# Ends of an attention on VectorE, two blocks of the next projection at a time, and a batch norm's variance summed beside the attention

## The chip, the cores and the metric

The kernel runs on one core of a Trainium2 chip. The metric is the device time of one launch in microseconds. The time before is the median of three runs. All stages below run one after the other on the same core; its engines are TensorE (PE in the profile, with its weight loads PEld), VectorE (DVE), ScalarE (ACT), GpSimd (POOL) and SyncE (SP), which issues most of the plain transfers.

## The reference

A graph of N = 3327 nodes has 512 features a node (x) and a sparse 0/1 adjacency matrix (adj). Four layers follow, each as `x = x + layer(relu(layernorm(x)))`:

```
layer 0   attention (8 heads of 64), then batch norm over the nodes (mean, var), scale, shift, relu
layer 1   mean over neighbours (mask @ h / degree), two linear maps, concatenated, a third, relu
layer 2   attention (8 heads of 64), elu
layer 3   attention (8 heads of 64), elu

attention: Wh = h W;  e[i,j] = leaky_relu(s[i] + d[j]) where adj[i,j], else minus infinity
           out[i] = softmax_j(e[i,:]) @ Wh, head by head
batch norm: mean and var of the attention's output over all nodes, a value for each of 512 columns
```

## The kernel before

The nodes are padded to 3328 and held as 26 blocks of 128 rows (NB = 26). Since the adjacency is sparse, each group of 64 destination nodes (52 groups, two to a block) keeps a list of the source nodes that it needs, rounded up to chunks of 128. The table CAPS has the number of chunks of each group, 22 for the first down to 4 for the last; 359 chunks in all. Every stage that reads neighbours gathers the 359 chunks by an indirect DMA that GpSimd issues (`gather`, L1165), one chunk at a time, into tiles named rows (attentions) or z_rows (layer 1).

**Attention** (`attend`, L1170). The groups are cut into 135 units of two or three chunks. For a unit VectorE makes mx (L1266: the larger of two factors of the exponential, one from PSUM and one from the gathered rows) and wgt (L1273: mx times the 0/1 mask), and TensorE multiplies wgt with the gathered rows into facc (L1287). In the first attention VectorE also unpacks the mask's bits ("on", L1252) and ScalarE turns them into the mask (L1258). The gathered rows have six buffers, and the gathers of a unit are issued one unit ahead in the program; GpSimd may run further ahead, up to what the buffers allow.

When a group's last unit has gone through, its end is worked off in steps, one step for each following unit (`ending`, L1201): ScalarE copies facc to sums (L1215), VectorE takes the reciprocal of the row sums (rd, L1219), ScalarE scales eight pieces of 64 columns into the block's output (L1225, named bn_y in layer 0 and fhp later). After a block's second group come the steps of `finish`: for layers 2 and 3 the elu (fin_e, fin_x, L1314 to L1320).

At each unit `later()` moves every pending end on by one step and then calls `tick()`, the work beside the attention. PE, VectorE and ScalarE run in the order in which the program calls them (`manual_schedule`); GpSimd's and SP's order is made by the framework's scheduler.

**Beside the first attention** (`beside`, L1339). Each tick does a small piece: first two products of layer 1's weights, then the sum of the attention's output over the nodes, a block at a time, as a matmul with ones (bmean_ps, L1374). After the attention the mean is taken (L1376). The variance follows in a stage of its own (L1398 to L1407): for two blocks at a time VectorE subtracts the mean (bn_d), ScalarE squares, TensorE sums into var_ps; bn_var is the result. Then come the batch norm's scale and shift, the layer norm of layer 1 and one of its linear maps.

**Layer 1** gathers the 359 chunks again (z_rows), sums them on TensorE (sage_acc, L1522) and finishes a block in `ending` (L1459).

**Beside layers 1 and 2** the projection of the following attention is made, a block at a time, by the class `Following` (L740): `norm` (layer norm, ScalarE sums, squares and scales; the result is ln_h), then `rest_by_rows` (used beside layer 1, where the vectors `ab` are given) or `rest` (beside layer 2): transposes (p_ps), relu to hT, the product with the score weights (p_sd), the product with the weights (p_wh, L866), eight ScalarE scalings into v_row (L870), which goes to the table in memory, and the transposed scores (p_tr to r_row), which go to r_dram. `tick` advances the block in front by two steps when two are waiting, else by one:

```
for _ in range(min(2, len(self.ready))):
    while self.ready and next(self.ready[0]) is None:
        self.ready.pop(0)
```

All PSUM tiles of `rest` share one tag of two buffers. When the units of the attention are through, `while ends: later()` works off the last ends, and `proj.drain()` (L1534) the last blocks of the projection. The next attention's first gather needs the whole table.

Of the kernel before, what the change touches and what calls it, by code (L numbers as in the profile page):

```python
# [23 lines left out]
F32 = mybir.dt.float32  # L24
# [7 lines left out]
AF = mybir.ActivationFunctionType  # L32
# [6 lines left out]
P = 128  # L39
# [13 lines left out]
HALF = 64  # L53
BATCH = 4
WB = 16
LNB = 5
ROW = H * (F + 1) + H
UNIT = 3
# [681 lines left out]
class Following:  # L740
# [3 lines left out]
    def __init__(self, tc, cs, N, wl, W, WA, table, r_dram, pool, psum, pb=1, ab=None):  # L744

        self.__dict__.update(locals())
        nc = tc.nc
        if ab is not None:
            self.ab = pool.tile([P, 2, D], F32, name=f"ab{wl}")
            for k, a in enumerate(ab):  # L750
                nc.sync.dma_start(self.ab[:, k, :], a.partition_broadcast(P))
        self.NB = table.shape[0] // P
        self.Wt = pool.tile([P, KC, D], F32, name=f"fWt{wl}")
        nc.sync.dma_start(self.Wt, W.rearrange("(kc p) o -> p kc o", p=P))
        self.hs = pool.tile([P, self.NB, KC], F32, name=f"hs{wl}")
        self.early, self.ready = [], []

    def begin(self, c, xt):
        self.early.append(self.norm(c, xt))

    def tick(self):
        for _ in range(min(2, len(self.ready))):
            while self.ready and next(self.ready[0]) is None:
                self.ready.pop(0)
        for g in list(self.early):
            hx = next(g)
            if hx is not None:
                self.early.remove(g)
                self.ready.append((self.rest if self.ab is None else self.rest_by_rows)(*hx))
# [3 lines left out]
            self.tick()  # L773

    mean = Projection.mean

    def norm(self, c, xt):
        nc, pp, cs = self.tc.nc, self.pool, self.cs
# [62 lines left out]
    def rest(self, c, hx):  # L841
        nc, pp, WA, wl = self.tc.nc, self.pool, self.WA, self.wl
        tp = self.psum.tile([P, KC, P], F32, name="p_ps", tag="p_ps", bufs=self.pb)
        for kc in range(KC):
            nc.tensor.transpose(tp[:, kc, :], hx[:, kc * P : (kc + 1) * P], self.cs["ident"])
        hT = pp.tile([P, KC, P], F32, name="hT", tag="hT", bufs=2)
        for kc in range(KC):
            nc.scalar.activation(hT[:, kc, :], tp[:, kc, :], AF.Relu, accum_out=self.hs[:, c, kc : kc + 1])
        yield True
        self.mean(c, hT)  # L850
        sd = self.psum.tile([P, BANK], F32, name="p_sd", tag="p_ps", bufs=self.pb)
        for kc in range(KC):
            nc.tensor.matmul(sd[:, : 2 * H], hT[:, kc, :], WA[wl][:, kc, :], start=(kc == 0), stop=(kc == KC - 1))
        row = pp.tile([P, ROW], F32, name="v_row", tag="v_row", bufs=2)
        V = row[:, : H * (F + 1)].rearrange("p (h f) -> p h f", f=F + 1)
        d = sd[:, H : 2 * H]
        nc.scalar.activation(V[:, :, F : F + 1], d.rearrange("p (h o) -> p h o", o=1), AF.Exp)
        nc.scalar.activation(row[:, H * (F + 1) :], d, AF.Exp, scale=-0.8, bias=self.cs["down"])
        sf = pp.tile([P, H], F32, name="s_col", tag="s_col", bufs=2)
        nc.scalar.copy(sf, sd[:, :H])  # L860
        yield True

        nc.vector.tensor_scalar(sf, sf, -SMALL, SMALL, ALU.max, ALU.min)
        wh = self.psum.tile([P, D], F32, name="p_wh", tag="p_ps", bufs=self.pb)
        for kc in range(KC):
            nc.tensor.matmul(wh, hT[:, kc, :], self.Wt[:, kc, :], start=(kc == 0), stop=(kc == KC - 1))  # L866
        yield True
        rs = halves(nc, pp, self.cs, sf)
        for h in range(H):
            nc.scalar.mul(V[:, h, 0:F], wh[:, h * F : (h + 1) * F], V[:, h, F : F + 1])  # L870
        nc.sync.dma_start(self.table[c * P : (c + 1) * P, :ROW], row.bitcast(I32))
        yield True
        tr = self.psum.tile([2 * H, P], F32, name="p_tr", tag="p_ps", bufs=self.pb)
        nc.tensor.transpose(tr, rs(), self.cs["ident"])
        yield True
        rr = pp.tile([2 * H, P], F32, name="r_row", tag="r_row", bufs=2)
        nc.scalar.copy(rr, tr)
        n = P // GB
        nc.sync.dma_start(
            self.r_dram[c * n : (c + 1) * n, :, :, :].rearrange("g t h i -> (t h) g i"),  # L880
            rr.rearrange("h (g i) -> h g i", i=GB),
        )
        yield None
# [253 lines left out]
def sparse(ctx: ExitStack, tc: tile.TileContext, t: dict, out: bass.AP, WA, ls, cs, idx, rdeg, first):  # L1137
# [12 lines left out]
    def used(c):  # L1150
        return min(P, N - c * P)
# [15 lines left out]
        )  # L1167


    def attend(layer, table, r_dram, finish, tick=lambda: None, home=None):  # L1170

# [8 lines left out]
        with tc.tile_pool(name=f"fatt{layer}", bufs=2) as ap, tc.tile_pool(  # L1182
            name=f"facc_ps{layer}", bufs=2, space=PSUM
        ) as aps, tc.manual_schedule(engines={ET.PE, ET.DVE, ET.Activation}):
            rows, rrs, rbs, accs, ends = {}, {}, {}, {}, []

            def fetch(g):
                if g < ls.G:
# [12 lines left out]
            def ending(g, hps={}):  # L1201

                b, u = divmod(g, PG)
                if u == 0:
                    hps[b] = home[:, b, :] if home is not None else None
                    if home is None:
                        hp_ = ap.tile([P, D], F32, name="fhp", tag="hp", bufs=3)
                        hps[b] = hp_
                hp, o0 = hps[b], u * GB
                fin = finish(b, hp, ap)  # L1210
                if u == PG - 1:
                    next(fin)
                yield
                sm = ap.tile([P, sw], F32, name="sums", tag="sums", bufs=4)
                nc.scalar.copy(sm, accs.pop(g)[:, :sw])  # L1215
                sm = sm.rearrange("p (q x) -> p q x", x=F + 1)
                yield
                rd = ap.tile([P, hq, 1], F32, name="rd", tag="rd", bufs=4)
                nc.vector.reciprocal(rd, sm[:, :, F : F + 1])  # L1219
                yield  # L1220
                for v in range(PG):
                    mine = slice(v * GB, (v + 1) * GB)
                    for q in range(hq):
                        h = q * PG + v
                        nc.scalar.mul(hp[o0 : o0 + GB, h * F : (h + 1) * F], sm[mine, q, 0:F], rd[mine, q, :])  # L1225
                yield
                if u == PG - 1:
                    del hps[b]
                    yield from fin
# [31 lines left out]
            for i, (g, k0, n, begins, stops) in enumerate(units):  # L1261
# [31 lines left out]
                            )  # L1293
                if stops:
                    ends.append(ending(g))
            while ends:
                later()

    def following(lx, layer, wl, W, pb=1, ab=None):
# [30 lines left out]
    with ExitStack() as mx:  # L1330
# [8 lines left out]
        def beside(wp, wps):  # L1339
# [4 lines left out]
            for k, (wn, bn) in enumerate((("L1_WsT", "L1_gnn_b_self"), ("L1_WnT", "L1_gnn_b_nb"))):  # L1344
# [13 lines left out]
                for fc in range(KC):  # L1358
# [7 lines left out]
                    w = wp.tile([P, D], F32, name="fwx", tag="fwx", bufs=1)  # L1366
                    nc.scalar.copy(w, ps)
                    nc.sync.dma_start(wx_dram[k, fc, :, :], w)
            mean_ps = wps.tile([P, D], F32, name="bmean_ps", tag="beside", bufs=1)
            for c in range(NB):  # L1370
                while len(whole) <= c:
                    yield
                k = used(c)
                nc.tensor.matmul(mean_ps, ones[:k, :], y[:k, c, :], start=(c == 0), stop=(c == NB - 1))  # L1374
                yield
            nc.vector.tensor_scalar_mul(mean, mean_ps, 1.0 / N)  # L1376

        mean = mid.tile([P, D], F32, name="bn_mean")
        with tc.tile_pool(name="beside", bufs=1) as wp, tc.tile_pool(name="beside_ps", bufs=1, space=PSUM) as wps:
            bg = beside(wp, wps)  # L1380
# [14 lines left out]
        gps = mx.enter_context(tc.tile_pool(name="fsage_ps", bufs=2, space=PSUM))  # L1395
        two = [P, 2, D]
        with tc.tile_pool(name="fbn", bufs=1) as bp:
            var_ps = gps.tile([P, D], F32, name="var_ps", tag="n_ps")  # L1398
            for c in range(0, NB, 2):
                d = bp.tile(two, F32, name="bn_d", tag="bn_d", bufs=2)  # L1400
                nc.vector.tensor_tensor(d, y[:, c : c + 2, :], mean.unsqueeze(1).to_broadcast(two), ALU.subtract)
                nc.scalar.activation(d, d, AF.Square)
                for i in range(2):
                    k = used(c + i)
                    nc.tensor.matmul(var_ps, ones[:k, :], d[:k, i, :], start=(c + i == 0), stop=(c + i == NB - 1))
            var = bp.tile([P, D], F32, name="bn_var")
            nc.scalar.mul(var, var_ps, 1.0 / N)  # L1407
            nc.vector.tensor_tensor(gam, gam, rsqrt(nc, bp, cs, var, bufs=1)(), ALU.mult)
            nc.vector.tensor_tensor(mean, mean, gam, ALU.mult)
            nc.vector.tensor_tensor(bet, bet, mean, ALU.subtract)  # L1410
# [119 lines left out]
    with ExitStack() as l3:  # L1530
        at2 = proj
        proj = following(l3, 3, 2, t["L3_gnn_W"])
        attend(2, at2.table, at2.r_dram, elu_into(x2, x3, proj.begin), proj.tick)
        proj.drain()  # L1534
    attend(3, proj.table, proj.r_dram, elu_into(x3, out))


# [85 lines left out]
```

## Time and profile before

| what | us |
|---|---|
| median of three runs | 2559.43 (2559.01 to 2560.68) |
| the profiled execution: its own time | 2553.76 |
| its span | 2551.8 |
| lists and first projection | 0 to 319 |
| first attention | 319 to 806 |
| variance | 808 to 842 |
| batch norm, layer norm, first map of layer 1 | 842 to 930 |
| layer 1 | 930 to 1447 |
| second attention, with the last blocks of the next projection | 1447 to 2046 |
| third attention | 2046 to 2538 |

Busy time over the whole span: PE 1825.0 us (72%), VectorE 1852.3 (73%), ScalarE 1068.3 (42%), GpSimd 1387.4 (54%). These shares are means over stages that have different limits. What a part of the change is worth is read from the stage it lies in: which engine is full there, and which wait ends last. The profile counts a gather as busy for 0.95 us; what lies between two gathers shows as idle time before the second one, with the name of what ended it. "issue" there is time in which the engine waited for nothing that the profile shows.

### The profile page before, as it was taken

The numbers are of one execution on the slowest core, as the hardware profiler recorded it, in microseconds if no ns is written. First come the engines' busy times: TensorE is split into PE (matmuls) and PEld (weight loads), VectorE is DVE, ScalarE is ACT, GpSimd is POOL, SyncE is SP. The second block draws the span as 40 slices with busy tenths as digits, with TensorE's granted clock in tenths as the row PEclk, the third lists the DMA queues.
The fourth block names the chain that finished last, engine by engine and source line by source line (L and its number), as shares of the span: only waits on it lengthen the run. The fifth ranks groups of instructions, "written<-read, shape, count | busy, mean of one in ns | idle before, by whom it ended". The sixth has DMA issues, their size and how long they took to land.

```text
span 2551.8 us, 53690 instructions
## 1 busy us (share of the span) xinstructions
PE 1825.0 (72%) x21112; PEld 1161.8 (46%) x21112; DVE 1852.3 (73%) x2272; ACT 1068.3 (42%) x3810; POOL 1387.4 (54%) x1482
## 2 busy tenths in 40 slices
PE   3667756776677698889999657778878646566653
PEld 2444444454454342223333356656555435555543
DVE  7667579999997850222333499999877279999996
ACT  4553212333445332334455214667766601233444
POOL 1000176777772026777777277776554067777672
PEclk9767889988888899999999778897877787777787
DMA  8773198888783566788888478887665178888784
GB/s 326 288 263 123 43 296 276 280 281 260 241 253 95 191 217 198 234 247 260 254 267 255 125 223 242 235 240 232 199 200 177 39 215 232 236 238 243 232 238 123
DMA packets 189057, 562.57 MB, mean 220 GB/s; under 512 B 37764, under 2 KB 42304, under 8 KB 185470
## 3 DMA queue, kind: packets, MB, share of 16 engines
q0 software_dynamic: 115456, 404.86, 53.3%
q1 hardware_dynamic: 73342, 154.20, 17.0%
q8 instruction: 169, 2.77, 0.4%
q14 instruction: 90, 0.74, 0.1%
HBM read 499.26 MB, written 59.68 MB: 219 GB/s over the span
## 4 chain that ended last, share of the span: by engine, by line
PE 30%; DVE 24%; issue 13%; ACT 9%; DMA 8%; POOL 3%; DVEq 0%; SPq 0%; POOLq 0%; ACTq 0%
DVE mx L1266 12%; PE facc L1287 8%; DVE wgt L1273 8%; PE sage_acc L1522 4%; DMA z_rows<-h_dram,idx 4%; PE p_wh L866 4%; DMA rows<-table,idx 3%; PE n_ps L1471 3%; PE p_wh L808 3%; ACT fhp L1225 2%; POOL z_rows L1165 2%; PE s_ps L1445 2%; POOL rows L1165 1%; ACT bn_y L1225 1%; ACT v_row L870 1%
## 5 line engine op out<-in xcount | busy, mean ns | idle before, releaser
L1165 POOL DMA_INDIRECT rows<-table,idx x1077 | 1027.7, 954 | 580.0 <-issue 224.5
L1287 PE MATMUL facc<-rows,wgt 128*64 128x65 f32 x17232 | 722.5, 253 | 393.7 <-DVE wgt L1273 259.7
L1287 PEld LDWEIGHTS facc<-rows,wgt 128*64 128x64 f32 x17232 | 667.1, 165 | 518.2 <-DVE wgt L1273 310.5
L1266 DVE TENSOR_TENSOR mx<-r_bc,rows 128x1536 f32<-128x1536 f32 (+1 forms) x405 | 639.4, 1579 | 48.4 <-DMA fin_x<-fx 17.7
L1273 DVE TENSOR_TENSOR wgt<-mx,mask 128x1536 f32<-128x1536 f32 (+1 forms) x405 | 638.4, 1576 | 42.3 <-DVE mx L1266 1.0
L1165 POOL DMA_INDIRECT z_rows<-h_dram,idx x359 | 340.7, 949 | 273.7 <-ACT hT L1442 141.0
L1225 ACT ACTIVATE fhp<-sums,rd 64x64 f32<-64x64 f32 x832 | 219.9, 334 | 305.4 <-DVE rd L1219 302.0
L1522 PE MATMUL sage_acc<-z_rows,z_mask 128*64 128x512 f32 x718 | 209.8, 618 | 33.0 <-DMA z_rows<-h_dram,idx 32.6
L1258 ACT ACTIVATE mask<-on 128x192 uint8<-128x192 uint16 (+1 forms) x135 | 46.5, 345 | 325.3 <-DVE on L1252 321.8
L1086 POOL DMA_DIRECT2D list_b<-shift x12 | 6.0, 503 | 271.7 <-DVE shift L1040 271.5
L811 DVE TENSOR_TENSOR sd_pr<-p_wh,ab 128x1024 f32<-128x1024 f32 x26 | 31.8, 1225 | 141.4 <-PE p_wh L808 141.4
L1522 PEld LDWEIGHTS sage_acc<-z_rows,z_mask 128*64 128x64 f32 x718 | 52.2, 137 | 156.2 <-issue 77.6
L680 PE MATMUL wh_ps<-fWt,hT 128*128 128x512 f32 x208 | 123.3, 748 | 0.0
L866 PE MATMUL p_wh<-fWt,hT 128*128 128x512 f32 x208 | 117.2, 714 | 1.4 <-ACT s_col L860 1.4
L1225 ACT ACTIVATE bn_y<-sums,rd 64x64 f32<-64x64 f32 x416 | 109.5, 333 | 2.4 <-DVE rd L1219 0.5
L1503 ACT CAST z_mask<-mask 128x128 f32<-128x128 uint8 (+1 forms) x196 | 52.7, 284 | 118.7 <-PE sage_acc L1522 117.5
L1476 DVE TENSOR_TENSOR s_o<-n_ps,bn_y 128x512 f32<-128x512 f32 x26 | 17.9, 690 | 116.2 <-PE n_ps L1471 116.2
L1215 ACT COPY sums<-facc 128x260 f32<-128x260 f32 x156 | 56.6, 363 | 104.7 <-DMA rows<-table,idx 77.7
L1471 PE MATMUL n_ps<-fWx,aT 128*128 128x512 f32 x208 | 98.7, 608 | 0.0
L808 PE MATMUL p_wh<-fWt,hT 128*128 128x512 f32 x208 | 96.9, 610 | 2.0 <-DVE hT L699 1.9
L1445 PE MATMUL s_ps<-fWx,hT 128*128 128x512 f32 x208 | 93.5, 603 | 3.4 <-ACT hT L1442 3.4
L1198 PE MATMUL r_bc<-r_two,fones 2*128 2x512 f32 x156 | 89.1, 575 | 6.6 <-DMA r_two<-r_dram 3.6
(213 smaller groups left out, 2146.3 us busy)
## 6 DMA issues: line engine op xcount, KB each, us to landing
adj_i<-in_adj SPq DMA_DIRECT2D x26, 1664.0 KB
table<-v_row SPq DMA_DIRECT2D x78, 264.0 KB
rows<-table,idx POOLq DMA_INDIRECT x1077
fin_x<-fx SPq DMA_DIRECT2D x52, 256.0 KB
ln_x<-in_x SPq DMA_DIRECT2D x26, 256.0 KB
bn_x<-in_x SPq DMA_DIRECT2D x13, 512.0 KB
fx<-bn_x SPq DMA_DIRECT2D x13, 512.0 KB
fsage_x<-fx SPq DMA_DIRECT2D x26, 256.0 KB
```

The costliest lines, as they stand in the source:

```text
L680: nc.tensor.matmul(wh, hT[:, kc, :], self.Wt[:, kc, :], start=(kc == 0), stop=(kc == KC - 1))
L808: nc.tensor.matmul(wh, hT[:, kc, :], self.Wt[:, kc, :], start=(kc == 0), stop=(kc == KC - 1))
L866: nc.tensor.matmul(wh, hT[:, kc, :], self.Wt[:, kc, :], start=(kc == 0), stop=(kc == KC - 1))
L1165: nc.gpsimd.indirect_dma_start(out=dst, out_offset=None, in_=src[:, :], in_offset=bass.IndirectOffsetOnAxis(ap=idx[:, k : k + 1], axis=0))
L1198: nc.tensor.matmul(rb, ones[0:2, :].bitcast(F32R), rrs.pop(g).bitcast(F32R), start=True, stop=True)
L1225: nc.scalar.mul(hp[o0 : o0 + GB, h * F : (h + 1) * F], sm[mine, q, 0:F], rd[mine, q, :])
L1266: nc.vector.tensor_tensor(mx[:, :n], rbs[g].unsqueeze(1).to_broadcast(full), gt[:, :n, H * (F + 1) : ROW].unsqueeze(3).to_broadcast(full), ...
L1273: nc.vector.tensor_tensor(wt[:, :n], mx[:, :n], mk.unsqueeze(2).to_broadcast(full), ALU.mult)
L1287: nc.tensor.matmul(accs[g][v * GB : (v + 1) * GB, q * (F + 1) : (q + 1) * (F + 1)], wt[:, k, h, :], gt[:, k, h * (F + 1) : (h + 1) * (F + 1)],
L1445: nc.tensor.matmul(ps, hT[:, kc, :], Wx[:, 0, kc, :], start=(kc == 0), stop=(kc == KC - 1))
L1471: nc.tensor.matmul(ps, aT[:, kc, :], Wx[:, 1, kc, :], start=(kc == 0), stop=(kc == KC - 1))
L1522: nc.tensor.matmul(acc[u * GB : (u + 1) * GB, :], m, z, start=f, stop=l)
```

## The change

There are four parts.

1. **Ends after the last unit.** Once all units of an attention are through (`over`), an end that has not begun yet is done by VectorE alone: the reciprocal straight from facc in PSUM, and two products of 64 rows by 256 columns into the output, in place of ScalarE's copy and eight scalings. Ends that are already under way go on as before. This holds for all three attentions.
2. **Two blocks at a time.** After the last unit of the second attention the projection of the third is told to `hurry`: the three PSUM banks of mx become its banks (one each for p_sd, p_wh and p_tr), a tick moves two blocks by one step each, VectorE makes v_row in one instruction instead of ScalarE in eight, and the remaining norms use `norm_by_columns`. The drain is now part of the attention's loop, and so in the program's order.
3. **Norm by columns.** `norm_by_columns` does the layer norm on VectorE with bn_stats, bn_aggr and one tensor_scalar; it takes one step less than `norm`. All 26 blocks beside layer 1 use it.
4. **Variance beside the first attention.** `beside` sums, in one PSUM tile, the output (lower 64 rows) and the squares of its distance from a shift (upper 64 rows). The shift is the mean of the first eight blocks (NSHIFT); GpSimd subtracts it, ScalarE squares, TensorE sums, one step of each in a tick. Up to four blocks are under way. At the end the mean and the variance are put together from the two sums. The variance stage is gone.

```
@@ class Following @@
     def begin(self, c, xt):
-        self.early.append(self.norm(c, xt))
+        self.early.append((self.norm_by_columns if self.spare is not None or self.ab is not None else self.norm)(c, xt))
+    def bank(self, shape, name, k):
+        if self.spare is not None:
+            return self.spare[: shape[0], k, : shape[1]]
+        return self.psum.tile(shape, F32, name=name, tag="p_ps", bufs=self.pb)
     def tick(self):
+        if self.spare is not None:
+            for g in self.ready[:2]:
+                if next(g) is None:
+                    self.ready.remove(g)
+            self.step()
+            return
...
+    def norm_by_columns(self, c, xt):
+        nc.vector.bn_stats(st, xt)
+        nc.vector.bn_aggr(mv, st)
+        step = rsqrt(nc, pp, cs, mv[:, 1:2])
+        yield
+        y = step()
+        hx = pp.tile([P, D], F32, name="ln_h", tag="ln_h", bufs=3)
+        nc.vector.tensor_scalar(hx, xt, mv[:, 0:1], y, ALU.subtract, ALU.mult)
+        yield c, hx
...
@@ rest @@
-        for h in range(H):
-            nc.scalar.mul(V[:, h, 0:F], wh[:, h * F : (h + 1) * F], V[:, h, F : F + 1])
+        if self.spare is not None:
+            nc.vector.tensor_tensor(
+                V[:, :, 0:F], wh.rearrange("p (h f) -> p h f", f=F), V[:, :, F : F + 1].to_broadcast([P, H, F]), ALU.mult
+            )
+        else:
+            for h in range(H):
+                nc.scalar.mul(V[:, h, 0:F], wh[:, h * F : (h + 1) * F], V[:, h, F : F + 1])
...
@@ attend: ending @@
+                if over:
+                    sm = accs.pop(g)[:, :sw].rearrange("p (q x) -> p q x", x=F + 1)
+                    rd = ap.tile([P, hq, 1], F32, name="rd", tag="rd", bufs=4)
+                    nc.vector.reciprocal(rd, sm[:, :, F : F + 1])
+                    for v in range(PG):
+                        mine = slice(v * GB, (v + 1) * GB)
+                        nc.vector.tensor_tensor(
+                            hp[o0 : o0 + GB, :].rearrange("p (q v f) -> p q v f", v=PG, f=F)[:, :, v, :],
+                            sm[mine, :, 0:F], rd[mine].to_broadcast([GB, hq, F]), ALU.mult,
+                        )
...
@@ attend: after the units @@
-            while ends:
+            over.append(True)
+            if beside is not None:
+                mx = aps.tile([P, UNIT, H, GB], F32, name="mx", tag="mx", bufs=1)
+                beside.hurry(mx.rearrange("p k h i -> p k (h i)"))
+            while ends or (beside is not None and beside.busy()):
                 later()
@@ beside @@
-            for c in range(NB):
-                while len(whole) <= c:
-                    yield
-                nc.tensor.matmul(mean_ps, ones[:k, :], y[:k, c, :], start=(c == 0), stop=(c == NB - 1))
-                yield
-            nc.vector.tensor_scalar_mul(mean, mean_ps, 1.0 / N)
+            while w < NB:
+                n += 1
+                if squared and squared[0][0] < n:
+                    _, d = squared.pop(0)
+                    nc.tensor.matmul(ps[hi, :], ones[:k, hi], d[:k, :], start=(w == 0), stop=(w == NB - 1))
+                    w += 1
+                elif m < len(whole):
+                    nc.tensor.matmul(ps[lo, :], ones[:k, lo], y[:k, m, :], start=(m in (0, NSHIFT)), stop=(m in (NSHIFT - 1, NB - 1)))
+                    m += 1
+                    if m == NSHIFT:
+                        taken(shift, lo, 1.0 / (NSHIFT * P))
+                if made and made[0][0] < n - 1:
+                    _, d = made.pop(0)
+                    nc.scalar.activation(d, d, AF.Square)
+                    squared.append((n, d))
+                if m >= NSHIFT and v < m and v < w + 4:
+                    d = wp.tile([P, D], F32, name="bn_d", tag="bn_d", bufs=4)
+                    nc.gpsimd.tensor_tensor(d, y[:, v, :], shift, ALU.subtract)
+                    made.append((n, d))
+                    v += 1
+                yield
+            taken(mean, lo, 1.0 / N)
+            nc.vector.scalar_tensor_tensor(mean, shift, float(NSHIFT * P) / N, mean, ALU.mult, ALU.add)
+            nc.vector.tensor_tensor(shift, mean, shift, ALU.subtract)
+            nc.vector.tensor_tensor(shift, shift, shift, ALU.mult)
+            taken(d, hi, 1.0 / N)
+            nc.vector.tensor_tensor(var, d, shift, ALU.subtract)
...
@@ batch norm @@
-            for c in range(0, NB, 2):
-                nc.vector.tensor_tensor(d, y[:, c : c + 2, :], mean.unsqueeze(1).to_broadcast(two), ALU.subtract)
-                nc.scalar.activation(d, d, AF.Square)
-                for i in range(2):
-                    nc.tensor.matmul(var_ps, ones[:k, :], d[:k, i, :], start=(c + i == 0), stop=(c + i == NB - 1))
-            nc.scalar.mul(var, var_ps, 1.0 / N)
@@ second attention @@
-        attend(2, at2.table, at2.r_dram, elu_into(x2, x3, proj.begin), proj.tick)
-        proj.drain()
+        attend(2, at2.table, at2.r_dram, elu_into(x2, x3, proj.begin), proj.tick, beside=proj)
```

`taken` copies 64 rows of the PSUM tile to both halves of an SBUF tile, two ScalarE instructions.

## The prediction

> **What bounds the kernel now.** I read the busy time by stage first, then GpSimd's own queue, then the ends of the stages, because the change works only beside the first attention, on the norms, and at the ends. The busy time by stage (start:end, length, then busy us and count of TensorE, its weight loads, VectorE, ScalarE and GpSimd; granted clock, DMA share, GB/s):
>
> ```profile
> 319.00:806.00 487.00, 327.50 (x5926) 238.51 (x5926) 452.76 (x459) 174.09 (x613) 341.28 (x359) 0.87 0.82 260
> 808.00:846.00 38.00, 27.73 (x52) 9.72 (x52) 19.08 (x19) 15.68 (x16) 0.00 (x0) 0.91 0.00 0
> 930.00:1404.00 474.00, 436.54 (x1401) 159.21 (x1400) 127.89 (x243) 192.81 (x752) 340.72 (x359) 0.99 0.78 241
> 1998.00:2046.00 48.00, 26.30 (x75) 13.94 (x70) 5.94 (x21) 27.28 (x113) 0.00 (x0) 0.75 0.09 32
> ```
>
> The first attention is VectorE's: 452.8 of 487 us. From 808 to 846 the variance runs alone, with no gather. From 1998 to 2046 the second attention ends: no engine is busy for more than 57% of it, so a chain of waits sets its length. The 70% that GpSimd shows in the first attention misleads. Its timeline there (start, length, in brackets the idle time before and what ended it):
>
> ```profile
> 561.64 0.95 POOL L1165 DMA_INDIRECT rows<-table,idx  x1 [0.30 <-issue]
> 562.89 0.95 POOL L1165 DMA_INDIRECT rows<-table,idx  x1 [0.30 <-issue]
> 564.14 0.94 POOL L1165 DMA_INDIRECT rows<-table,idx  x1 [0.30 <-PE facc L1287]
> ```
>
> A gather starts every 1.25 us, 0.95 busy and 0.30 that nothing fills. 359 of them make 449 us of the 487, so GpSimd is nearly as full as VectorE. By the waits from 557 to 801, it sat 37.5 us in such gaps and only 15.1 us waiting for facc to free a buffer. In the stage from 930 to 1404 the same 449 of 474 us make it one of two bounds, with TensorE.
>
> The end of the second attention, in the chain that ended last (start, length, what):
>
> ```profile
> 2006.11 5.48 PE p_wh L866 x8
> 2011.61 1.75 ACT v_row L870 x8
> 2013.38 1.06 ACT fhp L1225 x4
> 2014.47 1.05 ACT fhp L1225 x4
> 2015.54 0.30 ACT ln_s L792
> ```
>
> Each of the last blocks waits for the one ahead of it: its projection on TensorE, then 16 ScalarE scalings of 64 columns, then the next block's layer norm. The last block's row of scores leaves ScalarE at 2044.16.
>
> **What the Trainium skill says.** "GPSIMD Engine Reference", 3.1 Elementwise: a two-input operation on GpSimd takes some 2.6 cycles an element at 1.2 GHz, 1.96 times VectorE's time. The trace has no such operation to check it by. "SBUF — State Buffer", Who interferes with whom: a VectorE instruction with two SBUF inputs contends with a GpSimd instruction that reads SBUF; one with at most one SBUF input does not. The trace agrees: gathers beside mx and wgt (one input in PSUM) stay at 0.95, while the one at 569.14, beside the two-input "on", takes 1.06. The same section: tensor_scalar can use both ports and then holds GpSimd off. The trace fits so far as the 128x512 tensor_scalar rs_h takes 0.43 us where a 128x512 tensor_tensor takes 0.69; no gather ran beside it.
>
> **The change part by part**, in the time frame of before.
>
> 1. The variance stage goes. Before, bn_var is ready at 841.74. After, the last product still ends at 802.13. VectorE then ends the last group itself: 0.18 for the reciprocal and two half-width products of some 0.4 each (from the 0.69), to 803.1. ScalarE does one square (0.6, from the 1.06 for twice the width) and the scalings of the group ahead (2.14), from 801.4 to 804.2. What follows is serial: subtraction on GpSimd 1.1, square 0.6, matmul 1.1 (807.1), two ScalarE copies for the mean 1.2, three VectorE passes of 0.69 and the variance pass 0.7, to about 810.5; the two copies of d lie beside those passes. **Gain 31.2.** Bounds 27 and 33.
>
> 2. GpSimd beside the first attention. In the changed kernel's instruction order GpSimd does 187 gathers, four subtractions, 7 gathers, two, 2 gathers, one, 6, one, 6, one, and then one after every 10 or 12 gathers; three stand behind the last gather. The 187th ends at 563.8 now. From there on it has 172 gathers x 1.25 = 215 and 23 subtractions. One is 512 x 2.6 / 1.2 GHz = 1.11 (estimate from the GPSIMD page) and the 0.30 of a gather: 1.41, so 32.4 in all. The last gather ends at 563.8 + 215 + 32.4 = 811.2. Its landing takes 4.15 (the chain has 5.10 from a gather's start, less 0.95), so the last mx starts at 815.4 instead of 798.4: **loss 17.0**. The lead of 9.2 us that GpSimd has now (789.1 to 798.4) is spent, and the bound of the stage passes to GpSimd. Bounds: at VectorE's 0.69 and no gap, 0.5; at 0.69 x 1.96 + 0.30 = 1.65, 22.5; and "on", blocked by a subtraction a third of the time, can add 8. What a subtraction waits for costs nothing more: it stands 6 to 10 gathers behind the place where the program asks for it, so the scalings and the matmul that it needs are older than the facc that the next gather needs anyway. If that cover fails, the gathers queued behind it start late, up to one unit, 4 us, once. The 26 squares (16 us) and 26 more matmuls (some 30 us) lie in idle time, ScalarE's 313 and TensorE's 160 us of this stage; on the path they would cost their 46. SP gets no transfer more.
>
> 3. The end of the second attention, three blocks left, by the changed order. The transposes of block 23 start at 2001.85 as now, hT to 2003.65, p_sd to 2005.6; p_wh has a bank of its own and follows at once, 5.2 us, to 2010.8. Meanwhile ScalarE ends its last group (2005.8; VectorE the other at 2004.0), exp and add to 2007.1, and VectorE has block 24 normed by 2009.8; its transposes run from 2010.8 to 2011.9. TensorE then waits for r_half, queued on VectorE behind v_row and the last block's norm, to 2013.1. p_tr, p_sd and p_wh of block 24 end at 2020.5. Transposes, hT and the mean's column of block 25 end at 2023.4, its p_sd and p_wh at 2030.5, then v_row, r_half, p_tr and r_row, 1.4: 2031.9 for 2044.16. **Gain 12.2**, bounds 4 and 16. It is no halving: the 1.9 + 5.2 us of TensorE a block stay serial, and they are late next. The banks are mx's, free since the last wgt.
>
> 4. The end of the third attention, by its timeline now:
>
> ```profile
> 2532.65 0.35 ACT L1215 COPY sums<-facc 128x260 f32<-128x260 f32 x1
> 2533.25 2.13 ACT L1225 ACTIVATE fhp<-sums,rd 64x64 f32<-64x64 f32 x8 [0.25 <-DVE rd L1219]
> ```
>
> Copy, reciprocal and scalings end at 2535.4. VectorE would have the same at 2532.4, and ScalarE is free for the exp at 2532.74. **Gain 2.7**, bounds 2 and 3.
>
> 5. The norms from 930 to 1404 move to VectorE, which is 27% busy there: 26 x (0.67 for bn_stats + 0.17 + 0.43) = 33 us, hidden beside TensorE and GpSimd. What ScalarE is rid of is worth nothing, as it is 41% busy. But each two-port tensor_scalar can hold GpSimd off by up to 0.43 in a stage that GpSimd bounds: 26 x 0.43 = 11 at most, 0 at least; **loss 3**. At the end of that stage p_wh of block 24 now stands ahead of the last n_ps, which eats the step that the shorter norm saves: 0, bounds -3 and 3.
>
> Sum: -31.2 + 17.0 - 12.2 - 2.7 + 3.0 = **-26.1**. The profiled execution took 2553.76 (the span of 2551.8 and 2.0 around it), so it becomes 2527.7. The median of the three runs shown, 2559.43, lies 5.7 above it; I forecast 2559.4 - 26.1 = **2533**. About what a measurement of this kernel can tell from no change is 0.2%, 5.1 us.
>
> **The rivals**, each from the gains of 46.1 (31.2 + 12.2 + 2.7).
> - GpSimd's new work is nearly free, because it fits into the gaps and the waits for buffers. For it: the 15.1 us of such waits. Against it: 23 places of even 1 us need more. Then step 2 costs 0.5 and step 5 nothing: 2559.4 - 45.6 = 2514.
> - The upper price, 22.5 and "on" blocked for 8, and step 5 at 8: 2559.4 - 46.1 + 38.5 = 2552.
> - Slower: each subtraction waits out a 1.76 us mx or wgt for the read port, so its place is 1.41 + 1.76 = 3.17. Step 2 then costs 23 x 3.17 - 15.4 = 57.5, and 2559.4 - 46.1 + 57.5 + 3 = 2574. It decides from 23 c - 15.4 = 48 on, c = 2.8 us. Against it: gathers of 0.95 beside mx and wgt, though these read no more than indices.
> - The change doesn't do what it says: block 24's norm comes too late and the last blocks stay serial. Step 3 then gives 4: 2541, inside the main case.
>
> **How the numbers follow.** Main case 0.60 (2522 to 2543); free GpSimd 0.18; upper price 0.14, of which 0.04 within 0.2%; slower 0.08, of which 0.01 within it. So faster 0.88, same 0.05, slower 0.07. The range, 2513 to 2551, leaves out the slower rival and half of the upper price.
>
> **What would show it.** Right: about 12 us from the last mx of the first attention to bn_var; from 565 on gathers 1.25 apart with few waits for facc, and VectorE idle before mx until DMA rows; a subtraction near 1.1 us; p_wh of the last blocks some 10 us apart. Wrong: VectorE as full as now up to the last unit (step 2 too dear); subtractions of 2.8 us, or mx and wgt above 1.76 (too cheap); z_rows gathers longer and TensorE waiting for them (step 5 too cheap).

## The result, and the profile after

The changed kernel takes **2537.7 us** (median of four runs, 2537.07 to 2537.99) against 2559.83 for the kernel before (four runs): 0.9915 of the time, 95% interval 0.9899 to 0.9932. Forecast were 2533, in a range of 2513 to 2551, with 0.88 for faster. The profiled execution took 2537.07 with a span of 2535.3. The spans differ by only 16.5 us, because before's profiled execution was 6.1 below its median and this one lies 0.6 below its own.

One thing told of the kernel before has to be put right: the PSUM tiles of the projection share one tag, but it has two buffers only beside layer 1. Beside the second attention, where step 3 plays, it has one.

Busy time by stage of the changed kernel, with the columns as before (start:end, length, TensorE, its weight loads, VectorE, ScalarE, GpSimd, clock, DMA share, GB/s): the first attention, what follows it up to bn_var, layer 1's gathers, the end of the second attention.

```profile
322.00:825.00 503.00, 348.04 (x5978) 241.60 (x5978) 468.24 (x461) 188.32 (x631) 377.05 (x385) 0.87 0.81 251
819.00:832.00 13.00, 6.34 (x95) 3.09 (x89) 5.99 (x11) 9.09 (x26) 2.55 (x2) 0.86 0.01 1
919.60:1399.10 479.50, 448.43 (x1401) 159.24 (x1401) 166.82 (x315) 139.27 (x591) 343.22 (x359) 0.99 0.77 238
1992.00:2031.00 39.00, 25.75 (x146) 14.54 (x142) 11.01 (x32) 16.60 (x76) 0.00 (x0) 0.78 0.11 43
```

The stage from 808 to 846 has become 13 us. The first attention is longer, and VectorE still looks like its bound (468 of 503 us). Layer 1's gathers took 474 and take 479; the 48 us at the end of the second attention are 39. Measured between the same events in both traces:

| step | from, to | before | after | difference | forecast |
|---|---|---|---|---|---|
| 1 | last mx of the first attention to bn_var | 43.38 | 12.92 | -30.5 | -31.2 |
| 2 | first mx to last mx | 467.83 | 484.74 | +16.9 | +17.0 |
| 3 | last wgt of the second attention to last r_row | 49.48 | 38.97 | -10.5 | -12.2 |
| 4 | last wgt of the third attention to the last fin_x | 8.72 | 6.58 | -2.1 | -2.7 |
| 5 | first to last gather of layer 1, and from the last one's end to the last r_row | 473.44, 41.59 | 479.37, 42.18 | +6.5 | +3.0 |
| | sum | | | -19.7 | -26.1 |

The first gather came 2.75 us later (322.18 for 319.43), in code that the change leaves alone; in other profiles of the same code it came between 318.3 and 325.4.

**GpSimd beside the first attention.** All 26 subtractions, by the tile bn_d (duration least/median/most in ns, first and last start in us):

```profile
L1464 POOL TENSOR_TENSOR bn_d<-bn_y,bn_shift x26: 1254/1278/1294, 566.5 to 823.7; 128x512 f32<-128x512 f32 x26
```

1.28 us where I took 1.11 from the Trainium skill ("GPSIMD Engine Reference", 3.1 Elementwise); the measurement decides. In the timeline (start, length, engine, line; in brackets idle time before it) one of them lies so:

```profile
802.79 0.94 POOL L1208 DMA_INDIRECT rows<-table,idx  x1 [0.30 <-PE facc L1347]
...
803.75 1.28 POOL L1464 TENSOR_TENSOR bn_d<-bn_y,bn_shift 128x512 f32<-128x512 f32 x1
...
804.17 1.02 DVE L1312 TENSOR_TENSOR on<-rows,fbit 128x128 uint16<-128x128 uint16 x1
...
805.19 0.96 POOL L1208 DMA_INDIRECT rows<-table,idx  x1 [0.16 <-issue]
```

From gather to gather it is 2.40 us, where it is 1.25 without a subtraction: the place costs 1.15, less than the instruction itself, as it starts 0.02 after the gather's end and only 0.16 of idle time follows, together less than the usual 0.30. And "on", which takes 0.28 at this width, takes 1.02 and ends 0.16 after the subtraction. Fifteen "on" of this attention ran beside a subtraction; they took 0.67 to 2.56. That is the contention that the skill's page "SBUF — State Buffer", Who interferes with whom, describes for two SBUF inputs beside a GpSimd instruction that reads SBUF. Was the queue or this hold the cause of the 16.9 us? The waits of VectorE from 577 to 818 (us in total, times, longest) seem to speak for the hold:

```profile
DVE on L1312 <- DMA rows<-table,idx: 2.4, 2, 1.5
DVE wgt L1333 <- PE r_bc L1242: 0.5, 1, 0.5
```

VectorE hardly waits for rows; it is busy 230.4 of 241.1 us there, against 217.9 of 226.2 before (the changed kernel, then the kernel before; columns as above):

```profile
577.10:818.20 241.10, 167.34 (x2849) 116.64 (x2847) 230.43 (x230) 111.35 (x375) 186.78 (x188) 0.85 0.76 230
572.20:798.40 226.20, 151.93 (x2832) 116.70 (x2829) 217.91 (x229) 98.43 (x354) 157.02 (x166) 0.84 0.78 242
```

Busy time that a hold stretches looks like work in such a table: "on" took 33.4 us of it, against 21.2 before, and these 12.2 us are most of what was lost. GpSimd's own waits speak for the queue, as none is longer than the 0.3 that lies between any two gathers (before, single ones lasted over 3):

```profile
POOL rows L1208 <- issue: 33.3, 115, 0.3
POOL rows L1208 <- PE facc L1347: 5.2, 17, 0.3
```

To tell the two apart, experiments were needed.

**The end of the second attention**, TensorE's timeline:

```profile
1999.38 1.89 PE L891 MATMUL mx<-WA,hT 128*128 128x16 f32 x8 [0.46 <-ACT hT L886]
2003.72 6.55 PE L904 MATMUL mx<-fWt,hT 128*128 128x512 f32 x8 [2.45 <-ACT s_col L898]
...
2012.66 1.49 PE L891 MATMUL mx<-WA,hT 128*128 128x16 f32 x8
2014.76 6.16 PE L904 MATMUL mx<-fWt,hT 128*128 128x512 f32 x8 [0.61 <-ACT r_row L920]
...
2023.25 1.04 PE L891 MATMUL mx<-WA,hT 128*128 128x16 f32 x8 [1.15 <-DVE hT L700]
2024.90 3.70 PE L904 MATMUL mx<-fWt,hT 128*128 128x512 f32 x8 [0.61 <-ACT r_row L920]
```

Two blocks do go at once: p_wh (L904) starts 11.0 and 10.1 us apart. But each waits for ScalarE, 2.45, 0.61 and 0.61 us, which I had not foreseen.

**The end of the third attention**, in place of ScalarE's copy and eight scalings:

```profile
2517.73 0.18 DVE L1261 RECIPROCAL rd<-facc 128x4 f32<-128x4 f32 x1
2517.94 0.88 DVE L1264 TENSOR_TENSOR fhp<-facc,rd 64x256 f32<-64x256 f32 x2
```

### The profile page after: what moved, and what is told of

The parts are those of the page before. It is cut to its first block, busy times and chain, and to the rows that moved or that the text cites. A ratio compares the mean times of both kernels' runs of the same rounds, so it can differ in the third digit from the quotient of the medians.

```text
span 2535.3 us, 53563 instructions
## 1 busy us (share of the span) xinstructions
PE 1848.6 (73%) x21112; PEld 1172.1 (46%) x21112; DVE 1901.8 (75%) x2355; ACT 996.7 (39%) x3581; POOL 1427.6 (56%) x1508
## 5 line engine op out<-in xcount | busy, mean ns | idle before, releaser
L1347 PE MATMUL facc<-rows,wgt 128*64 128x65 f32 x17232 | 744.1, 256 | 346.4 <-DVE wgt L1333 241.2
L1347 PEld LDWEIGHTS facc<-rows,wgt 128*64 128x64 f32 x17232 | 690.0, 168 | 484.5 <-DVE wgt L1333 292.8
L1333 DVE TENSOR_TENSOR wgt<-mx,mask 128x1536 f32<-128x1536 f32 (+1 forms) x405 | 638.4, 1576 | 41.9 <-ACT bn_y L1285 0.5
L1612 PE MATMUL sage_acc<-z_rows,z_mask 128*64 128x512 f32 x718 | 220.2, 620 | 30.8 <-DMA z_rows<-h_dram,idx 30.7
L846 PE MATMUL p_wh<-fWt,hT 128*128 128x512 f32 x208 | 98.6, 618 | 2.1 <-DVE hT L700 1.9
L904 PE MATMUL p_wh<-fWt,hT 128*128 128x512 f32 x184 | 99.9, 691 | 0.0
L1242 PE MATMUL r_bc<-r_two,fones 2*128 2x512 f32 x156 | 94.8, 611 | 7.0 <-DMA r_two<-r_dram 3.4
L1044 PE MATMUL words_ps<-wsel,adj_b 128*128 128x8 bf16 x676 | 24.8, 168 | 88.7 <-DVE adj_b L1026 48.4
```

What stands on the lines that cost most here:

```text
L1242: nc.tensor.matmul(rb, ones[0:2, :].bitcast(F32R), rrs.pop(g).bitcast(F32R), start=True, stop=True)
L1333: nc.vector.tensor_tensor(wt[:, :n], mx[:, :n], mk.unsqueeze(2).to_broadcast(full), ALU.mult)
L1347: nc.tensor.matmul(accs[g][v * GB : (v + 1) * GB, q * (F + 1) : (q + 1) * (F + 1)], wt[:, k, h, :], gt[:, k, h * (F + 1) : (h + 1) * (F + 1)],
L1612: nc.tensor.matmul(acc[u * GB : (u + 1) * GB, :], m, z, start=f, stop=l)
```

## The experiments

Twelve kernels ran in three groups of four; the kernels of a group share a chip, and the first two groups ran on the same one. In the first two groups the kernel before took 2946.9 us (2941.9 to 2962.2) and 2955.8 (2943.6 to 2964.3), in the third 2557.4 (2552.9 to 2562.8). So times are compared within a group, and stages only where the chips agree. "The stretch" is from the 70th mx to the last mx of the first attention: 226.20 before, 241.04 after.

**A chip on which TensorE sets the pace.** First the variance without GpSimd arithmetic, as the mean square less the squared mean:

```
-    nc.gpsimd.tensor_tensor(d, y[:, v, :], shift, ALU.subtract)
-    made.append((n, d))
+    nc.scalar.activation(d, y[:, v, :], AF.Square)
+    squared.append((n, d))
...
+    nc.vector.tensor_tensor(shift, mean, mean, ALU.mult)
```

> The changed kernel with the shift left out of the variance: ScalarE squares the attention's output itself, TensorE sums the squares, and the variance is the mean square less the squared mean. GpSimd gets no arithmetic; all else is as changed. In the changed kernel the stretch from the 70th mx of the first attention to its last mx takes 241.0 us, before it took 226.2. Both theories of those 14.8 us (GpSimd's queue is full; VectorE's two-input 'on' is blocked by the subtraction at the shared port) expect 225 to 228 here, and with the shorter end (one subtraction of 1.28 and two VectorE passes of 0.69 less) a median near 2518. If instead the loss came from the 26 squares on ScalarE and the 26 extra matmuls on TensorE, which stay, the stretch stays near 241 and the median near 2535.

Measured: 2893.82, 0.9798 of before (0.9758 to 0.9838); stretch 278.7. Second, a fill in the subtraction's place:

```
+    for width in (D, D, 384):
+        nc.gpsimd.memset(d[:, :width], 0.0)
```

> As the run without GpSimd arithmetic (variance from the plain squares), but at each place of the subtraction GpSimd fills the same buffer with zeros by three memsets of 512, 512 and 384 columns, some 1.3 us together, which read nothing from SBUF. If GpSimd's full queue is what costs (rate: 1.25 us a gather and 1.3 to 1.4 us a block beside it), the stretch from the 70th to the last mx stays at 236 to 243 us and VectorE's lost time shows as waits for gathered rows. If the block at the shared port is what costs, 'on' keeps 0.35 us and the stretch falls to 226 to 229.

Measured: 2892.9, 0.9804 (0.9763 to 0.9844); stretch 283.1. Third, the subtraction issued twice:

> The changed kernel with each subtraction done twice on GpSimd, into the same buffer. By the theory that GpSimd's queue paces the stretch, 23 more places of 1.28 to 1.4 us make it 30 to 32 us longer: 271 to 273 us from the 70th to the last mx, the median near 2569. By the theory of the blocked 'on' each further subtraction blocks one more unit's 'on' by at most the 0.7 us seen: 241 + 12, the median near 2551.

Measured: 2916.45, 0.9881 (0.9841 to 0.9922); stretch 290.4. Fourth, the old norm beside layer 1:

```
-    (self.norm_by_columns if self.spare is not None or self.ab is not None else self.norm)
+    (self.norm_by_columns if self.spare is not None else self.norm)
```

> The changed kernel, but the 26 layer norms beside layer 1 are done as before, on ScalarE (norm by columns only for the last two blocks of the second attention). In the changed kernel the gathers of layer 1 take 479.4 us from the first start to the last end, before 473.4. If the norm on VectorE costs those 5.9 us (two-port ln_h holding off the gathers, and the changed order of TensorE at the end), this run shows 473 to 475 and a median some 6 lower than the changed kernel, near 2532. If they come from elsewhere, 479 stays.

Measured: 2912.95, 0.9865 (0.9822 to 0.9908); stretch 280.9 with the change's own variance, layer 1's gathers 575.6.

None of the expected lengths came, as another engine was the bound. Then the changed kernel on this chip, and two of the edits once more:

> The changed kernel itself, as the base for the kernels beside it on the same chip. On the chip of the first runs (kernel before at 2559.8 us): 2537.7 us, stretch from the 70th masked product to the last of the first attention 241 us, end of the second attention (last weight product to last r_row) 39.0 us, gathers of layer 1 479 us. If this is again a chip on which the kernel before takes some 2947 us: about 2913 us, and TensorE, not VectorE or GpSimd, is what the first attention waits for.

Measured: 2902.63, 0.9818 (0.9772 to 0.9863); stretch 281.5, end of the second attention 36.5, layer 1's gathers 559.8.

> No subtraction on GpSimd: ScalarE squares y itself, and the variance is the mean square less the squared mean. The first of the earlier runs, on a chip where TensorE set the pace, could not tell. Where VectorE and GpSimd set it: stretch 225 to 228 us against 241 in the changed kernel, 'on' not over 0.4 us, time 13 to 16 us below the changed kernel. If not the subtraction but the squares on ScalarE or the sums on TensorE cost the 15 us, the stretch stays at 238 to 242 us.

Measured: 2891.29, 0.9782 (0.9740 to 0.9825); stretch 278.8.

> As the run without GpSimd arithmetic, but GpSimd fills a tile with zeros in the subtraction's place, in pieces of 512, 512 and 384 columns: about as long in GpSimd's queue, but with one operand and no reading. My theory (the shared port: VectorE's 'on' is held while a subtraction reads) expects 'on' at 0.35 us, the stretch at 226 to 231 us and the time within 4 us of the run without arithmetic. The rival (GpSimd's queue itself is full, so that every 1.4 us of it is a later gather) expects waits for gathered rows, a stretch of 236 to 243 us and the time within 4 us of the changed kernel.

Measured: 2891.91, 0.9789 (0.9736 to 0.9842); stretch 281.4.

With the subtraction, without it, with fills: 281.5, 278.8, 281.4. These runs could not decide. What bounds this chip stands in TensorE's waits over the whole span, of the changed kernel here:

```profile
PE facc L1347 <- issue: 408.8, 734, 14.2
```

and on the first chip:

```profile
PE facc L1347 <- DVE wgt L1333: 241.2, 167, 14.4
PE facc L1347 <- issue: 81.3, 42, 3.4
```

In the timeline of the changed kernel here, 48 products that take 1.62 us at best come in handfuls:

```profile
675.36 0.41 PE L1347 MATMUL facc<-rows,wgt 128*64 128x65 f32 x6 [0.39 <-issue]
676.83 0.32 PE L1347 MATMUL facc<-rows,wgt 128*64 128x65 f32 x3 [1.07 <-issue]
677.57 0.22 PE L1347 MATMUL facc<-rows,wgt 128*64 128x65 f32 x1 [0.42 <-issue]
678.29 0.32 PE L1347 MATMUL facc<-rows,wgt 128*64 128x65 f32 x2 [0.51 <-issue]
```

TensorE waits there for nothing that the trace shows. VectorE then waits for facc, 41.9 us before mx from 640 to 890 (0.2 in the stretch on the first chip), and so does GpSimd, 42.0 us: it has time to spare. The second subtraction costs 9 us of the stretch, where 20 of them at 1.28 would be 26. What makes this chip slower I did not settle. On it the old norm is no remedy for layer 1: 575.6 us against 559.8 with the norm by columns in the changed kernel, and 553.7 to 563.2 in the other runs with it.

**Three PSUM tiles for the ends** settled step 3 all the same, as the products into facc end soon after it begins:

```
-    return self.spare[: shape[0], k, : shape[1]]
+    return self.spare[k][: shape[0], : shape[1]]
...
-    beside.hurry(mx.rearrange("p k h i -> p k (h i)"))
+    one = aps.tile([P, H * GB], F32, name="r_bc", tag="r_bc", bufs=2)
+    two_ = aps.tile([P, H * GB], F32, name="r_bc", tag="r_bc", bufs=2)
+    beside.hurry((one, mx[:, 0, :, :].rearrange("p h i -> p (h i)"), two_))
```

> The three PSUM banks of the hurried ends are three tiles instead of slices of one tile. My theory (the projection p_wh of the next block waits because a slice of a tile that another slice's reader still holds counts as taken) expects p_wh without the waits of 2.45, 0.61 and 0.61 us ahead of it, the end of the second attention at 34 to 36.5 us against 39.0, and the time 2.5 to 5 us lower. The rival (ScalarE's own order, with s_col and r_row ahead of the next hT, is what p_wh waits for) expects 38 to 39 us and the time within 1 us.

Measured: 2888.23, 0.9781 (0.9734 to 0.9829); the end of the second attention takes 30.1 us against 36.5. TensorE's timeline:

```profile
2262.69 1.89 PE L891 MATMUL r_bc<-WA,hT 128*128 128x16 f32 x8 [0.46 <-ACT hT L886]
2264.42 6.09 PE L904 MATMUL mx<-fWt,hT 128*128 128x512 f32 x8
...
2272.89 0.96 PE L891 MATMUL r_bc<-WA,hT 128*128 128x16 f32 x8
2273.71 3.68 PE L904 MATMUL mx<-fWt,hT 128*128 128x512 f32 x8
...
2279.72 1.04 PE L891 MATMUL r_bc<-WA,hT 128*128 128x16 f32 x8 [1.20 <-DVE hT L700]
2280.61 3.68 PE L904 MATMUL mx<-fWt,hT 128*128 128x512 f32 x8
```

p_wh follows p_sd with no wait, where the changed kernel waits 2.45, 0.61 and 0.61 us on this chip too. The three slices of the first version lie in three banks too, and TensorE's order is the same: what it waited for was that ScalarE let go of p_sd and p_tr, which are parts of the same tile. The rival, ScalarE's own order, is out. The gain of 6.4 us is more than the 2.5 to 5 expected: 4.1 lie between the starts of p_sd and of p_wh, and 1.5 in p_wh itself. Its eight products take between 3.68 and 6.55 us in the last three blocks of these traces, for a reason that I did not settle; kernels with the same end took 36.5 to 37.7 on this chip. The whole time is 14.4 us below the changed kernel's, but single runs of one kernel lie over 20 us apart here.

**Less for TensorE.** To bring VectorE and GpSimd back to the front, the middle one of three chunks was left out of the products in the first attention, so that the sums are no longer the attention's; a small constant keeps them from zero:

```
     for k in range(n):
+        if layer == 0 and n == 3 and k == 1 and g < ls.G - 1:
+            continue
...
-    nc.scalar.copy(sm, accs.pop(g)[:, :sw])
+    nc.scalar.activation(sm, accs.pop(g)[:, :sw], AF.Identity, bias=eps_t)
```

> The changed kernel with less for TensorE in the first attention: of a unit of three gathered blocks the middle block's 16 products are left out (not in the last group of rows), so that VectorE and GpSimd, not TensorE, set its pace also on the chip of the last runs; a small constant is added to the sums so that none is zero. The output is then not the reference's. Base for the next two. Expected as on the first chip: a stretch from the 70th masked product to the last of the first attention of 238 to 246 us (TensorE-bound it was 281), with 'on' again up to 2 us long beside a subtraction.

Measured: 2531.18, 0.9893 (0.9870 to 0.9916); stretch 237.7. This group ran on a chip like the first, where the edit would not have been needed, but it does no harm: the stretch is near the changed kernel's 241.0. "On" was held less than expected, by 1.3 us at most.

> The same with no subtraction on GpSimd and the variance from plain squares. If the subtraction is what cost 15 us on the first chip: stretch 225 to 230 us, 11 to 16 us below the light base. If it was the squares and sums: the same as the light base within 3 us.

Measured: 2517.56, 0.9845 (0.9823 to 0.9868), 13.6 us below the light base; stretch 226.6. The squares and sums stay: 16 of the 26 squares lie in the stretch, 21 in the light base, on a ScalarE that is busy for half of it.

> The same, with GpSimd filling a tile with zeros (512, 512 and 384 columns) in the subtraction's place, the variance from plain squares. Shared port: 'on' 0.35 us, stretch within 4 us of the light kernel without GpSimd arithmetic. GpSimd's queue full: waits of VectorE for gathered rows, stretch 8 to 16 us above that kernel, close to the light base. In between, with 'on' at 0.35: each has a part.

Measured: 2537.05, 0.9918 (0.9898 to 0.9939); stretch 242.4, 15.8 above the kernel without. Its "on" (ns least/median/most) and the waits of VectorE in the stretch:

```profile
L1312 DVE TENSOR_TENSOR on<-rows,fbit x65: 279/348/360, 581.2 to 819.5; 128x192 uint16<-128x192 uint16 x42, 128x128 uint16<-128x128 uint16 x23
```

```profile
DVE on L1312 <- DMA rows<-table,idx: 14.0, 19, 1.5
```

This is the run that decides. The fills hold up no "on" (0.36 at most), and the stretch is as long as with subtractions: now VectorE openly waits 14.0 us for rows. The fills take up the queue much as the subtractions do. From the 187th gather on, the intervals in which they stand exceed 1.25 by 30.9 us in all; those of the subtractions do so by 26.9 in the changed kernel and by 27.6 in the light base. Many fills stand singly between two gathers and cost 0.30 to 0.41 each; later three stand together, as one stop of 1.60:

```profile
709.14 0.95 POOL L1208 DMA_INDIRECT rows<-table,idx  x1 [0.30 <-issue]
710.09 1.60 POOL L1465 MEMSET bn_d<- 128x512 f32 x3
712.00 0.95 POOL L1208 DMA_INDIRECT rows<-table,idx  x1 [0.31 <-PE facc L1349]
```

The light base says the same. The subtractions fall beside other instructions there, "on" takes only 2.4 us more than before, and VectorE waits openly:

```profile
DVE on L1312 <- DMA rows<-table,idx: 7.8, 12, 1.9
```

Still its stretch is 11.1 us longer than without subtractions. So **GpSimd's queue is the main cause**, not the squares, the sums or the hold. When "on" is held, VectorE spends in it the time that it would else spend waiting for rows: hold and waits together are 14.6 us in the changed kernel, 10.2 in the light base and 14.1 with fills. The theory of the shared port, which I had taken up after seeing the profile, fell as the main cause; the forecast's mechanism stood. What the hold can cost beyond that is bounded by the run with fills: from the last gather's end to the last mx it is 6.99 us in the changed kernel and 4.44 with fills, and the intervals of gathers with nothing between them exceed 1.25 by 2.75 and 0.94 us in all. That leaves the hold 4.4 of the 14.8 us at most.

**Both remedies**, with the whole computation: no subtraction and three tiles.

> The whole computation: no subtraction on GpSimd (variance from plain squares) and three PSUM tiles for the hurried ends, together. On the chip of the last runs, where these two alone gave 2891.3 and 2888.2 us against 2902.6 for the changed kernel: the end of the second attention 30 to 32 us (6.4 less), the time 2877 to 2890 us, below both, as they lie in different stages. On the first chip I would expect 2514 to 2520 us.

Measured: **2508.88** us (2507.99 to 2509.70), 0.9812 of before (0.9793 to 0.9831). Busy time in the stretch:

```profile
570.60:796.70 226.10, 163.31 (x2836) 117.01 (x2835) 217.82 (x229) 106.70 (x370) 155.79 (x165) 0.84 0.79 241
```

226.1 us, as before the change, and the end of the second attention takes 32.2. The time is below the 2514 to 2520 expected for such a chip. It beats the kernel before directly, and the changed one by its ratio, whose interval doesn't meet that of the changed kernel. Its variance is the mean square less the squared mean, which gives up the shift and so loses digits where a column's mean is large beside its spread.

## Why the prediction was right, point by point

- **Step 1** held: 30.5 for 31.2. The mean's copies come last, as forecast: they wait for the last sum (826.83), and VectorE's four passes follow to 831.08. The forecast's last terms (807.1, 1.2, three passes of 0.69 and one of 0.7) add up to 811.1, not to the 810.5 it gives, so that its own sum is 30.7.
- **Step 2** held in mechanism and in the end, 16.9 for 17.0, by terms that were off and cancel: that it came so close is luck. 23 subtractions stand among the last 172 gathers, as counted. From the 187th gather's end to the last one's it is 244.65 us, forecast 215 + 32.4 = 247.4, before 225.29. The place was taken at 1.11 + 0.30 = 1.41; it is 1.15, although the subtraction is dearer (1.28, some 1.85 times VectorE's 0.69), because no idle time is added: the 23 cost 26.9 us, not 32.4. Against it stand 2.75 us by which the other intervals exceed 1.25, which I had set to none, and the last mx, 6.99 after the gather's end and not 4.15. I also gave as a sign against step 2 that VectorE is as full as before up to the last unit. It was (230 of 241 us), and the step held: a wrong mark, since a held instruction counts as busy. For the same reason the sign for it, VectorE idle until rows, came to 2.4 us only. The upper price added 8 us for a blocked "on"; 12.2 came, but mostly in place of waits.
- **Step 3** was right in kind, 10.5 for 12.2. The term that failed is "p_wh has a bank of its own and follows at once": a bank, but not a tile. With three tiles the end is 6.4 us shorter on one chip, and 32.2 (both remedies) against 38.97 us on chips like the first, 4.7 of it between the starts of p_sd and p_wh. The forecast's 37.2 (2031.9 less 1994.68) without any such wait was thus 5 us too long in its other terms, which hid most of the miss. Of these 5, p_wh has 1.1 (14.5 us for three blocks with both remedies, 15.6 taken); the rest I did not trace.
- **Step 4**: 2.1 for 2.7. The two products and the reciprocal take 1.06 us.
- **Step 5** was mis-sized: 6.5 for 3.0. ln_h takes 0.546 us, not 0.43, and the gathers' excess over 0.946 grew from 1.1 to 3.6 us (19 took over 1.0, 11 of them beside ln_h): a hold of about the size that I had taken. The rest is in waits that were not in the sum. GpSimd's waits in that stage:

```profile
POOL z_rows L1208 <- PE p_tr L869: 13.4, 8, 2.0
```

  The row was not there before; waits for sage_acc shrank from 40.4 to 27.3 us meanwhile. That TensorE's new order makes the net 3 us is only argued: the old norm ran on the slower chip alone, where it cost time, so this stays open.
- **Rivals.** GpSimd's work nearly free, and a place of 3.17 behind each mx or wgt, are both out: the place is 1.15 and mx and wgt kept their 1.76. The upper price would have cost 22.5 in step 2. "The change doesn't do what it says" fell with p_wh 10 to 11 us apart.

The steps give 6.4 us less than forecast, mostly in steps 3 and 5. For the profiled execution the forecast was 2527.7, and 2537.07 came: 9.4 more, of which the later first gather has 2.75. The median came out only 4.7 above the forecast, because before's profiled execution lay 6.1 below its median and this one 0.6: that part is luck.

## What to carry to other kernels

Price work for an idle-looking engine by its queue: count the instructions between which it must fit, and compare with what the queue waits for today, not with its busy share. An instruction that is held counts as busy, so "still full" doesn't tell who sets the pace; a filler that takes up the queue about as long and reads nothing does. And slices of one PSUM tile, though in separate banks, waited here for each other's readers where separate tiles didn't; whether the framework or the chip makes them wait, these runs don't tell.

## What the runs showed of the hardware

- A subtraction of 128x512 on GpSimd takes 1.28 us, but between two gathers it costs 1.15, since the 0.30 that lies between gathers shrinks to 0.02 before it and 0.16 behind it. Three fills of zeros together cost 1.61 (2.86 from gather to gather), single ones 0.30 to 0.41.
- Beside a GpSimd subtraction VectorE's two-input "on" takes 1.02 us in place of 0.28, and up to 2.56; beside fills never over 0.36; mx and wgt (one input in PSUM) were not held at all (1.76 beside a subtraction too).
- The kernel before took 2557 us on one chip and 2947 and 2956 on another. On the slower one TensorE idled 409 us before the changed kernel's facc products with no releaser in the trace, against 81 where that kernel took 2538, at a granted clock of 0.794 and 0.838.
